# A four-layer image kernel on one core: the first scan chain's opening 160 steps interleaved with the tail of the gated layer

## The chip, the core and the metric

The kernel runs on one core of a Trainium2 chip, in one launch. The metric is the device time of that launch in microseconds, from the first to the last instruction on the core and the little that lies around it. Everything is in fp32.

The core has five engines that matter here. TensorE (PE, with its weight loads listed as PEld) multiplies matrices, VectorE (DVE) and ScalarE (ACT) work element by element, GpSimd (POOL) copies and adds, and SyncE (SP) issues nearly all the transfers. Each engine works through its own list of instructions in a fixed order.

## What is computed

Four residual layers on an input of 4 images, 48 channels, 256 x 256 pixels. Each layer adds f(groupnorm(x)) to x.

```python
# layer 0: channel attention; layer 1: gated tokens; layers 2 and 3: line scans
x = x + L0(_gn(x)); x = x + L1(_gn(x)); x = x + L2(_gn(x)); x = x + L3(_gn(x))

def step(w, b):                      # layers 2 and 3
    def f(carry, inp):
        nxt = inp + _conv1d(carry, w, b)      # 5 taps along the line, 48 -> 48 channels
        return (nxt, nxt)
    return f
_, d_rest = jax.lax.scan(step(down_w, down_b), d0, xs[1:])    # down the rows
_, u_rest = jax.lax.scan(step(down_w, down_b), u0, seq)       # up again
_, r_rest = jax.lax.scan(step(right_w, right_b), r0, ws[1:])  # to the right
_, l_rest = jax.lax.scan(step(left_w, left_b), l0, R[Ww - 2::-1])  # to the left
```

Layer 0 is a 1x1 and a 3x3 convolution, a 48 x 48 softmax attention over channels, and a projection. Layer 1 reinterprets the image as tokens of 48 numbers, applies two small dense products with GELUs, a layer norm, a 3x3 and a 1x1 convolution whose product gates half of the channels, and a last dense product. Layers 2 and 3 are chains: about a thousand line steps, each of which needs the result of the one before.

## The kernel before

`layers01` first forms the Gram products of layer 0 image by image, and from them folds attention and projection into one 3x3 convolution. This convolution is done in blocks of 16 rows, 16 blocks an image: `block(u)` gives six pieces, and one call of `conv()` (L631) runs three of them. The 16 blocks of image 0 run first; the other 48 are then mixed with the gated layer.

The gated layer (`gated_layer`, L649) works on 32 chunks, 8 an image, in a software pipeline: `tick(c)` (L906) finishes chunk c-2, works on chunk c and prepares chunk c+1. A tick calls `conv` four times, so two blocks go with a tick, until the list `todo` is empty. Before the ticks, four calls run two blocks ahead (L642). After `todo` is empty the remaining ticks are the lone gated chunks. In them `output` loads the residual x of the following chunk itself (L884, `load_x`, tile `xr`), where otherwise it comes at the head of the tick. All loads and stores of a chunk (`tok`, `xr`, `near`, the store at L889) go through SP's one queue.

`scans` then makes one generator for each of the two pairs of images. `chain(pair)` yields after each line step. `step` (L1059) is six matmuls in the source into two PSUM tiles, two VectorE additions that form the new line (`carry`), and two ScalarE writes (`keep`) into the slot that the input line came from. The first pass goes down 256 rows in eight groups of 32. Group n uses two slots, `halves[2n]` for the even rows and `halves[2n+1]` for the odd rows; a slot is 96 x 4096 floats, 1.5 MB, loaded in four transfers by `load_rows` (L1091) and then normalized in place by ScalarE at L1125. At the start of group n the list `halves` is filled up to index 2n+4 (L1142). When a group is finished its two slots are stored as `D[n]` (L1165).

Slots come from `take` (L1019) through a `Ring` of pools. `slots_a` has three buffers, in the memory that the convolution leaves; `slots_b` and `slots_c` have one each, in memory of the gated layer. The ring of pair 0 goes a, a, a, c, b and round again, so `halves[3]`, the odd rows of group 1, sits in c, and that is free only when the gated layer no longer uses it.

The order on each engine is fixed when the program is built. A planner walks through simulated time; among the instructions that are ready it takes the one with the lowest number, and numbers go up in the order in which the code emits. `tc.high_priority(offset=n)` sets the number back by n for what is emitted within it. `tc.issue_after(ins)` puts transfers in SP's queue behind `ins`, and waits for nothing else. `look` (L1033) is a tiny VectorE addition that is pinned in program order and reads a number written a few steps before. So the chains' first steps may move up among the lone gated chunks in two ways: as fill where the planner sees an engine free, or with a number that is set back. In the kernel before only the first two calls of `next(chains[0])` are set back (weights, the first two slots, then the first normalization and the loads of three more slots); the line steps have numbers after the gated layer's. Without a look go groups 0 and 1 of pair 0, layer 2 (L1159).

Of the kernel before, what the change touches and what calls it, by code (L numbers as in the profile page):

```python
# [1 line left out]

# [1 line left out]

# [12 lines left out]
B, C, H, W = 4, 48, 256, 256  # L17
# [4 lines left out]
R = 16  # L22
# [3 lines left out]
NK = W // (2 * KC)  # L26
LEAD = 4 * H - 32
# [32 lines left out]
class Coefs:  # L60


    def __init__(self, nc, pool, at, cst):
        self.nc, self.at = nc, at
        self.t = pool.tile([128, cst.shape[1]], F32, tag="cst", name="cst")
        nc.sync.dma_start(self.t, cst)
        self.eps = pool.tile([128, 1], F32, tag="eps", name="eps")
        nc.gpsimd.memset(self.eps, GN_EPS)
# [50 lines left out]
class Ring:  # L119


    def __init__(self, pools):
        self.pools = list(pools)

    def tile(self, *args, **how):
        self.pools.append(self.pools.pop(0))
        return self.pools[-1].tile(*args, **how)

# [2 lines left out]
def layers01(ctx, tc, x, x1, wqk, dwqk, wv, dwv, projT, temp, k, coef, coef1, gated, spare):  # L131
# [11 lines left out]
    nc = tc.nc  # L143
# [3 lines left out]
    p_small = ctx.enter_context(tc.tile_pool(name="a_ps", bufs=1, space=PSUM))  # L147
# [47 lines left out]
    halves = wp.tile([P, 2], F32, tag="halves", name="halves")  # L195
# [3 lines left out]
    w1 = wp.tile([P, 3, 3, P], F32, tag="w1", name="w1")  # L199
# [298 lines left out]
    banks = ctx.enter_context(tc.tile_pool(name="a_banks", bufs=5, space=PSUM))  # L498
# [63 lines left out]
    ends = []  # L562
# [68 lines left out]
    def conv():  # L631

        while ends:
            ends.pop(0)()
        if todo:
            u, q = todo.pop(0)
            if q == 0:
                made[u] = block(u)
            for piece in made[u][3 * q : 3 * q + 3]:
                piece()  # L640

    for _ in range(4):  # L642
        conv()
    for t in range(-1, n_ticks):
        for piece in tick(t, conv, not todo):
            piece()


def gated_layer(ctx, tc, banks, p_small, x1, x2, w1, w2, dw, ends, pw, cols, b2, k, coef1, coef2):  # L649

# [3 lines left out]
    nc = tc.nc  # L656
# [184 lines left out]
    def load_x(c, ip):  # L841

        if c >= len(items) or (c, ip) in xrs:
            return
        b, j = items[c]
        t = xrs[c, ip] = res.tile([P, 8, W], F32, tag=f"xr{ip}", name="xr")
        src = x1[b].rearrange("c (h w) -> c h w", w=W)[:, 2 * j * R : 2 * (j + 1) * R, :]
        src = src.rearrange("c (q i r) w -> i r c q w", i=2, r=2)
        for r in range(2):
            nc.sync.dma_start(t[r * C : (r + 1) * C], src[ip, r])  # L850

    def add_b2(c, ip):
        t = xrs[c, ip]
# [2 lines left out]
    def output(c, ip, alone):  # L856
# [27 lines left out]
        if alone:  # L884
            load_x(c + 1, ip)
# [76 lines left out]


@with_exitstack
def scans(ctx, tc, xs, out, wts, biases, dram, k, coefs, lead, spare):

# [10 lines left out]
    nc = tc.nc  # L979
# [7 lines left out]
    slots_a = pool("c_slot_a", 3)  # L987
    wp = pool("c_w", 1)
    work = pool("c_work", 1)
    slots_b = pool("c_slot_b", 1)  # L990
    slots_c = pool("c_slot_c", 1)
    slots_d = pool("c_slot_d", 5)
    p_small = pool("c_ps", 1, space=PSUM)
# [2 lines left out]
    sums = [spare, psum]  # L996
    zero = p_zero.tile([P, 1], F32, tag="zero", name="zero")
    nc.vector.memset(zero, 0.0)
    buffers = [Ring([slots_a] * 3 + [slots_c, slots_b]), Ring([slots_d] * 5)]
    NT = H // RT  # L1000
    NH = RT // 2
    CB = 2 * KC
# [19 lines left out]
    def chain(pair):  # L1022
# [10 lines left out]
        def look(place, fetched=None):  # L1033

            kept.append(place)
            old = [kept.pop(0)] if len(kept) > 3 else []
            for number in old + ([] if fetched is None else [fetched]):
                tc.keep_in_program_order(nc.vector.tensor_add(seen, zero, number))  # L1044

        def slot(name):
            return take(pair, f"{name}{pair}")

        def inner():
            return carry[at[0]][:, :, 1 : HP - 1]  # L1050
# [5 lines left out]
        def blocks(v):  # L1056
            return v.rearrange("p b (k w) -> p b k w", w=KC)
# [20 lines left out]
        def rows_view(t):  # L1078
            return t.rearrange("p (b k h w) -> p b k h w", b=2, k=NK, w=KC)
# [8 lines left out]
        def row(ts, r):  # L1088
            return rows_view(ts[r % 2])[:, :, :, r // 2, :]

        def load_rows(layer, n, r, t, k0, k1):  # L1091

            v = rows_view(t)
            for b in range(2):
                for q in range(2):
                    nc.sync.dma_start(
                        v[q * C : (q + 1) * C, b, k0:k1].rearrange("c k h w -> c k (h w)"),
                        xs[layer][pair][
                            r * C : (r + 1) * C, b, 2 * k0 + q : 2 * k1 - 1 + q : 2, n * NH : (n + 1) * NH, :
                        ].rearrange("c k h w -> c k (h w)"),  # L1100
                    )

        def layer_of(layer, first):
# [11 lines left out]
            for b in range(2):  # L1115
                t = home.tile([P, 2], F32, tag=f"biased{pair}{b}", name="biased", bufs=2)
# [5 lines left out]
            def norm(t, b):  # L1122
                v = by_batch(t)[:, b]
                g = biased[b]
                nc.scalar.activation(v, v, AF.Identity, bias=g[:, 1:2], scale=g[:, 0:1])  # L1125
# [10 lines left out]
            halves = list(first)  # L1136
            for n in range(NT):
                ahead_ = None
                for r in range(RT):
                    if r == 0:  # L1140
                        kept.clear()
                        while len(halves) < min(2 * n + 5, 2 * NT):  # L1142
                            t = slot("dn")
                            load_rows(layer, len(halves) // 2, len(halves) % 2, t, 0, NK)
                            halves.append(t)
                        if n + 1 < NT:
                            ahead_ = halves[2 * n + 2 : 2 * n + 4]
                    if ahead_ and r in (11, 14, 22, 25):
                        norm(ahead_[r // 22], r % 11 // 3)
                    inp = row(now, r)  # L1150

                    def keep(new, b):
                        nc.scalar.activation(inp[:, b], blocks(new[:, b]), AF.Identity, bias=bias[:, 0:1])  # L1153

                    if n == 0 and r == 0:
                        keep(inner(), slice(0, 2))
                    else:
                        step(layer, 0, inp, keep)
                    if pair or layer or n > 1:  # L1159

                        look(inp[:, 1, 0, 0:1])
                    yield
                if ahead_:
                    for r in range(2):
                        nc.sync.dma_start(D[n][r], now[r])  # L1165
                    now = ahead_
# [5 lines left out]
            for n in reversed(range(NT)):  # L1172
                ahead_ = None
                kept.clear()
                for r in reversed(range(RT)):
# [17 lines left out]
                    i = n * RT + r + 1  # L1193
# [9 lines left out]
                    else:  # L1203
                        step(layer, 0, place, keep)
                    look(place[:, 1, 0, 0:1])
                    yield
                    if n == 0 and r < 2:
# [63 lines left out]
            for n in range(NK):  # L1271
                ahead_ = None
                for w in range(CB):
# [27 lines left out]
                    if n + 1 < NK or w + 1 < CB:  # L1301
                        look(line[:, 1, 0:1], fetched[n * CB + w + 1][:, 1, 0:1])
# [91 lines left out]
            if layer == 0:  # L1394

                ends = []
# [14 lines left out]

        first = [slot("dn"), slot("dn")]
        for r in range(2):
            load_rows(0, 0, r, first[r], 0, NK)
        yield
        for layer in range(2):
            following = None
# [5 lines left out]
            first = following  # L1423

    def to_rows(pair, engines):
# [6 lines left out]
        for n in range(NY):  # L1432
# [9 lines left out]
            for half in range(2):  # L1442
# [12 lines left out]
                yield  # L1455

    chains = [chain(pair) for pair in range(NP)]

    with tc.high_priority(offset=1600):
        next(chains[0])  # L1460
    with tc.high_priority(offset=1400):
        next(chains[0])
    for i in range(1, lead):
        if i == lead - 2 * RT:
            next(chains[1])
        next(chains[0])
# [14 lines left out]
@with_exitstack  # L1481
def program(ctx, tc, a, out, at):
    nc = tc.nc
    const = ctx.enter_context(tc.tile_pool(name="const", bufs=1))
    dram = ctx.enter_context(tc.tile_pool(name="dram", bufs=1, space=DRAM))
    k = Coefs(nc, const, at, a["cst"])
    coefs = [
        [const.tile([P, 2], F32, tag=f"coef{layer}_{b}", name=f"coef{layer}_{b}") for b in range(B)]
        for layer in range(4)
    ]  # L1490
    spare = ctx.enter_context(tc.tile_pool(name="spare", bufs=2, space=PSUM))
    x1 = [dram.tile([C, HW], F32, tag=f"x1_{b}", name=f"x1_{b}") for b in range(B)]
    xs = [
        [dram.tile([P, 2, NK * 2, H // 2, KC], F32, tag=f"x{i}_{p}", name=f"x{i}_{p}") for p in range(NP)]
        for i in (2, 3)
    ]

    def gated(ctx, tc, banks, p_small):
        names = ("w1", "w2", "dw", "ends", "pw", "cols", "b2")
        return gated_layer(ctx, tc, banks, p_small, x1, xs[0], *(a[n] for n in names), k, coefs[1], coefs[2])  # L1500

    names = ("wqk", "dwqk", "wv", "dwv", "projT", "temp")
    layers01(tc, a["x"], x1, *(a[n] for n in names), k, coefs[0], coefs[1], gated, spare)
    scans(tc, xs, out, (a["c2w"], a["c3w"]), (a["c2b"], a["c3b"]), dram, k, coefs, LEAD, spare)


def _block_diag(m, n):
# [95 lines left out]
```

## Time and profile before

| what | value |
|---|---|
| device time, median of 3 runs | 8974.04 us (8972.58 to 8974.45) |
| the profiled execution's own time | 8983.88 us |
| its span, first to last instruction | 8982.1 us |
| PE busy | 8646.3 us, 96% |
| DVE, ACT, POOL busy | 4167.5, 3479.8, 1948.9 us |
| bytes moved by the transfer engines | 1390.64 MB, 155 GB/s over the span |
| scan matmuls L1067 | 48960 records, 5423.7 us busy |

Stages on the time line, with the line numbers that open and close them: the Gram products to about 1750 us, the convolution with the gated layer to about 3175 us (the last store of the convolution is issued at 3169.88 us), the lone gated chunks to about 3575 us, the scans to the end. The scan matmuls run from 3244.8 us.

How to read it: time that PE is not busy is what can be won, since PE's own work is the same in both kernels. A view by windows gives the busy time of each engine in a stretch, the mean TensorE clock that was granted there (PEclk, 1.00 is full), the share of the transfer engines that was busy, and the GB/s they moved. A scan matmul's record overlaps with its neighbours, so counts tell more than summed durations: where the chain runs alone 230 records fit in 25 us, which is 109 ns each, and a step has 12 records (48960 over 4080 steps), so 1.30 us.

### The profile page before, as it was taken

What the parts mean: (1) busy time and instruction counts of PE and PEld (TensorE: products, weight loads), DVE (VectorE), ACT (ScalarE), POOL (GpSimd) and SP (SyncE); (2) the same over time, 40 slices, a digit from 0 to 9 for tenths busy, and PEclk for the clock granted to TensorE, in tenths of its full rate; (3) what the DMA queues carried; (4) which work ended last, traced back from release to release, by engine and by line L of the source; (5) the groups of instructions that cost most, each with busy time, mean ns of one, the idle gap of its engine ahead of it and who ended that gap; (6) DMA issues with size and microseconds to landing.
All of it is one profiled execution on the core that took longest, in us unless ns stands there. A gap on an engine that the chain in (4) does not pass through costs nothing. (4 is left out here: it accounts for less than half of the span.)

```text
span 8982.1 us, 162711 instructions
## 1 busy us (share of the span) xinstructions
PE 8646.3 (96%) x62920; PEld 7223.1 (80%) x62920; DVE 4167.5 (46%) x15625; ACT 3479.8 (39%) x7023; POOL 1948.9 (22%) x3100
## 2 busy tenths in 40 slices
PE   6999999999999978999999999999999999999998
PEld 4777777533333335999999999999999999999998
DVE  3231110234555555445666444445666555444653
ACT  0010101123433455766601776666663003665610
POOL 0000000001111111001454000001445664101575
PEclk9999999999999988999999999999999999999998
DMA  7654323367888876765577664556656887867789
GB/s 152 132 125 94 74 61 77 82 140 160 173 181 182 182 165 162 168 138 143 155 190 190 152 139 120 141 135 141 169 146 175 216 220 181 198 172 191 210 176 183
DMA packets 1180233, 1390.64 MB, mean 155 GB/s; under 512 B 263184, under 2 KB 1107216, under 8 KB 1118784
## 3 DMA queue, kind: packets, MB, share of 16 engines
q1 hardware_dynamic: 1179360, 1379.90, 65.7%
q8 instruction: 493, 8.08, 0.4%
q14 instruction: 284, 2.33, 0.1%
q0 software_dynamic: 96, 0.33, 0.0%
HBM read 811.21 MB, written 509.61 MB: 147 GB/s over the span
## 5 line engine op out<-in xcount | busy, mean ns | idle before, releaser
L1067 PE MATMUL ps<-carry,w 96*96 96x128 f32 x48960 | 5423.7, 273 | 59.3 <-DVE carry L1071 29.1
L1067 PEld LDWEIGHTS ps<-carry,w 96*96 96x96 f32 x48960 | 5397.6, 163 | 95.0 <-issue 44.9
L1264 POOL COPY pre<-col 96x256 f32<-96x256 f32 x1020 | 657.5, 646 | 2682.2 <-DMA col<-last 1964.1
L1153 ACT ACTIVATE dn<-carry,b 96x128 f32<-96x128 f32 (+1 forms) x2044 | 769.0, 398 | 796.8 <-DVE carry L1071 789.0
L1291 ACT ACTIVATE lines<-carry,b 96x128 f32<-96x128 f32 (+1 forms) x2044 | 819.8, 402 | 583.9 <-DVE carry L1075 574.0
L1071 DVE TENSOR_TENSOR carry<-ps,dn 96x128 f32<-96x128 f32 x2280 | 653.2, 288 | 806.1 <-PE ps L1067 781.2
L1199 ACT ACTIVATE up<-carry,b 96x128 f32<-96x128 f32 x1792 | 719.5, 402 | 459.9 <-DVE carry L1071 459.6
L1075 DVE TENSOR_TENSOR carry<-ps,lines 96x128 f32<-96x128 f32 x2040 | 576.8, 286 | 562.8 <-PE ps L1067 552.9
L1075 DVE TENSOR_TENSOR carry<-ps,pre 96x128 f32<-96x128 f32 x2040 | 586.7, 288 | 457.6 <-PE ps L1067 402.4
L1071 DVE TENSOR_TENSOR carry<-ps,up 96x128 f32<-96x128 f32 x1792 | 516.0, 288 | 598.1 <-PE ps L1067 592.8
L1339 POOL TENSOR_TENSOR stage<-stage,carry 96x256 f32<-96x256 f32 x768 | 657.4, 857 | 470.4 <-DVE seen L1044 436.7
L581 PE MATMUL py<-x1n,wy 128*96 128x512 f32 x1536 | 703.1, 607 | 30.9 <-ACT x1n L541 28.4
L295 PE MATMUL acc<-xs,xt 128*96 128x288 f32 x2048 | 667.2, 408 | 0.0
L294 PE MATMUL acc<-xt 128*96 128x288 f32 x2048 | 666.8, 409 | 0.0
L581 PEld LDWEIGHTS py<-x1n,wy 128*96 128x96 f32 x1536 | 244.2, 165 | 454.7 <-issue 437.1
L279 DVE COPY xt<-pt 128x384 f32<-128x384 f32 x256 | 136.7, 555 | 849.0 <-PE pt L276 645.8
L261 ACT ACTIVATE xn<-raw,coef 96x2048 f32<-96x2048 f32 x64 | 133.7, 2095 | 987.0 <-PE pt L276 819.6
L296 PE MATMUL acc<-xt,xs 128*96 128x192 f32 x2048 | 502.1, 327 | 0.0
L296 PEld LDWEIGHTS acc<-xt,xs 128*96 128x96 f32 x2048 | 332.4, 165 | 154.5 <-issue 1.8
L295 PEld LDWEIGHTS acc<-xs,xt 128*96 128x96 f32 x2048 | 332.2, 165 | 151.4 <-issue 2.8
L604 DVE TENSOR_TENSOR y<-py,t 96x512 f32<-96x512 f32 x256 | 171.4, 678 | 593.3 <-PE py L590 584.4
L590 PE MATMUL py<-x2n,wy 64*96 64x512 f32 x1536 | 363.0, 601 | 0.0
(186 smaller groups left out, 5542.7 us busy)
## 6 DMA issues: line engine op xcount, KB each, us to landing
stage<-x SPq DMA_DIRECT2D x64, 1536.0 KB
dn<-x SPq DMA_DIRECT2D x240, 384.0 KB
R<-lines SPq DMA_DIRECT2D x60, 1536.0 KB
lines<-R SPq DMA_DIRECT2D x60, 1536.0 KB
D<-dn SPq DMA_DIRECT2D x56, 1536.0 KB
up<-D SPq DMA_DIRECT2D x56, 1536.0 KB
U<-up SPq DMA_DIRECT2D x224, 384.0 KB
col<-U SPq DMA_DIRECT2D x56, 1536.0 KB
```

Source lines behind the costliest of these rows:

```text
L294: nc.tensor.matmul(acc[0], lhsT=xt[:, h + 2, :], rhs=xt[:, here, :], start=first, stop=last)
L295: nc.tensor.matmul(acc[1], lhsT=xt[:, h + 2, :], rhs=xs[:, here, :], start=first, stop=last)
L296: nc.tensor.matmul(acc[2], lhsT=xs[:, h + 2, :], rhs=xt[:, past, :], start=first, stop=last)
L581: nc.tensor.matmul(ps, lhsT=held["w"][0][:, dx], rhs=x1n[:, 2 * c : 2 * c + 2, dx : dx + W], start=dx == 0, stop=False)
L1067: nc.tensor.matmul(ps, lhsT=w_sb[layer][:, way, j, :], rhs=old[:, i, j : j + W // 2], start=j == 0, stop=j == 2)
L1071: nc.vector.tensor_add(new[:, i].rearrange("p (k w) -> p k w", w=KC), ps.rearrange("p (k w) -> p k w", w=KC), inp[:, i])
L1075: nc.vector.tensor_add(new[:, i], ps, inp[:, i])
L1153: nc.scalar.activation(inp[:, b], blocks(new[:, b]), AF.Identity, bias=bias[:, 0:1])
L1199: nc.scalar.activation(place[:, b], blocks(new[:, b]), AF.Identity, bias=bias[:, 1:2])
L1264: nc.gpsimd.tensor_copy(t, cols_view(block)[:, :, w % 2, :, w // 2])
L1291: nc.scalar.activation(line[:, b], new[:, b], AF.Identity, bias=bias[:, 2:3])
L1339: nc.gpsimd.tensor_add(to, to, new)
```

## The change

Four things change together.

- The convolution runs eight calls (four blocks) ahead of the first tick, not four. It is thus done a tick earlier, and there are 13 lone ticks rather than 12.
- The steps of pair 0 in the first five groups (160 calls) have numbers set back by 1400, call by call.
- The first eleven slots of pair 0 all come from the three buffers of `slots_a`; only then does the ring go c, b, a, a, a. Eleven slots are `halves[0]` to `halves[10]`, so groups 0 to 4 need no memory of the gated layer.
- The first two slots' loads stand in SP's queue behind the load of x (`xr`, second half) of chunk 21, the third slot's behind that of chunk 22.

Looks now begin at group 5 of that pass, where they began at group 2.

```diff
 class Ring:
-    def __init__(self, pools):
+    def __init__(self, pools, first=()):
         self.pools = list(pools)
+        self.first = list(first)
     def tile(self, *args, **how):
+        if self.first:
+            return self.first.pop(0).tile(*args, **how)
         self.pools.append(self.pools.pop(0))
...
-    for _ in range(4):
+    for _ in range(8):
         conv()
...
         for r in range(2):
-            nc.sync.dma_start(t[r * C : (r + 1) * C], src[ip, r])
+            loads[c, ip] = nc.sync.dma_start(t[r * C : (r + 1) * C], src[ip, r]).ins
...
-    buffers = [Ring([slots_a] * 3 + [slots_c, slots_b]), Ring([slots_d] * 5)]
+    buffers = [Ring([slots_c, slots_b] + [slots_a] * 3, [slots_a] * 11), Ring([slots_d] * 5)]
...
+        def behind(n):
+            return nullcontext() if pair else tc.issue_after(loads[B * H // (2 * R) - 11 + n, 1])
...
-                            load_rows(layer, len(halves) // 2, len(halves) % 2, t, 0, NK)
+                            with behind(1) if layer == 0 and len(halves) == 2 else nullcontext():
+                                load_rows(layer, len(halves) // 2, len(halves) % 2, t, 0, NK)
...
-                    if pair or layer or n > 1:
+                    if pair or layer or n > 4:
                         look(inp[:, 1, 0, 0:1])
...
         for r in range(2):
-            load_rows(0, 0, r, first[r], 0, NK)
+            with behind(0):
+                load_rows(0, 0, r, first[r], 0, NK)
...
     with tc.high_priority(offset=1600):
         next(chains[0])
-    with tc.high_priority(offset=1400):
-        next(chains[0])
-    for i in range(1, lead):
+    for i in range(160):
+        with tc.high_priority(offset=1400):
+            next(chains[0])
+    for i in range(160, lead):
         if i == lead - 2 * RT:
             next(chains[1])
         next(chains[0])
```

More of the change, by code (lines that the diff above doesn't have):

```diff
@@ L1 @@
-from contextlib import ExitStack
+from contextlib import ExitStack, nullcontext
 import numpy as np
@@ L646, in layers01, with gated_layer @@
             piece()
-def gated_layer(ctx, tc, banks, p_small, x1, x2, w1, w2, dw, ends, pw, cols, b2, k, coef1, coef2):
+def gated_layer(ctx, tc, banks, p_small, x1, x2, w1, w2, dw, ends, pw, cols, b2, k, coef1, coef2, loads):
     nc = tc.nc
@@ L964, in scans @@
 @with_exitstack
-def scans(ctx, tc, xs, out, wts, biases, dram, k, coefs, lead, spare):
+def scans(ctx, tc, xs, out, wts, biases, dram, k, coefs, lead, spare, loads):
     nc = tc.nc
@@ L1496, in program @@
     ]
+    loads = {}
     def gated(ctx, tc, banks, p_small):
         names = ("w1", "w2", "dw", "ends", "pw", "cols", "b2")
-        return gated_layer(ctx, tc, banks, p_small, x1, xs[0], *(a[n] for n in names), k, coefs[1], coefs[2])
+        return gated_layer(ctx, tc, banks, p_small, x1, xs[0], *(a[n] for n in names), k, coefs[1], coefs[2], loads)
     names = ("wqk", "dwqk", "wv", "dwv", "projT", "temp")
     layers01(tc, a["x"], x1, *(a[n] for n in names), k, coefs[0], coefs[1], gated, spare)
-    scans(tc, xs, out, (a["c2w"], a["c3w"]), (a["c2b"], a["c3b"]), dram, k, coefs, LEAD, spare)
+    scans(tc, xs, out, (a["c2w"], a["c3w"]), (a["c2b"], a["c3b"]), dram, k, coefs, LEAD, spare, loads)
 def _block_diag(m, n):
```

## The prediction

> **What bounds the kernel now.** I read the page first, then windows around the place where the slices dip, then SP's list and PE's waits there.
>
> ```profile
> PE 8646.3 (96%) x62920; PEld 7223.1 (80%) x62920; DVE 4167.5 (46%) x15625; ACT 3479.8 (39%) x7023; POOL 1948.9 (22%) x3100
> ...
> PE   6999999999999978999999999999999999999998
> ```
>
> PE is the bound nearly everywhere; the 7 and the 8 cover 3144 to 3593 us, where the lone gated chunks run. The windows (columns: stretch, length, busy and count of PE, PEld, DVE, ACT, POOL, then granted clock, share of the DMA engines, GB/s) say how much is lost there:
>
> ```profile
> 1750.00:3175.00 1425.00, 1342.04 (x4783) 496.29 (x4782) 685.48 (x1167) 506.93 (x483) 176.89 (x408) 0.98 0.79 169
> 3175.00:3575.00 400.00, 315.71 (x1541) 169.63 (x1540) 230.54 (x502) 207.32 (x283) 71.19 (x77) 0.84 0.74 164
> 3575.00:4250.00 675.00, 674.38 (x6144) 673.27 (x6143) 332.84 (x1530) 456.08 (x1063) 34.75 (x54) 1.00 0.66 153
> ...
> 3175.00:3245.00 70.00, 35.50 (x127) 14.66 (x126) 25.12 (x56) 26.32 (x26) 11.11 (x11) 0.68 0.97 180
> 3245.00:3575.00 330.00, 280.21 (x1415) 154.97 (x1415) 205.42 (x446) 180.99 (x258) 60.08 (x66) 0.87 0.70 161
> ```
>
> PE idles 84.3 us in these 400 us: 34.5 before the chain's first step, 49.8 beside it. The clock is down too. After 3575 us the chain alone fills PE (674.38 of 675), so whatever steps are not done earlier cost their 1.30 us each there and no more: only idle time and slow clock can be won. The first hole is made in SP's queue:
>
> ```profile
> 3171.51 1.47 SPq L850 DMA_DIRECT2D xr<-x  x1
> 3173.08 23.71 SPq L1096 DMA_DIRECT2D dn<-x  x12
> 3196.83 4.25 SPq L850 DMA_DIRECT2D xr<-x  x3
> ```
>
> Twelve loads of three slots take 23.7 us of issuing and stand before the chunk's residual x. PE's waits in 3175 to 3250, then in 3250 to 3470, then in 3470 to 3580 (total, times, longest):
>
> ```profile
> PE pout L868 <- DVE y L879: 21.2, 1, 21.2
> PE ptok L751 <- POOL pairs L745: 9.7, 1, 9.7
> ```
> ```profile
> PE ptok L751 <- DVE y L879: 16.3, 5, 3.5
> ```
> ```profile
> PE ps L1067 <- DVE carry L1071: 16.2, 7, 4.0
> ```
>
> The first two are that missing x, and token loads behind it. The third comes once a tick. The last is the chain itself standing at PE's head: at 3481 us the odd rows of group 1 are just loaded and being normalized, and everything behind that step on PE waits too.
>
> **What the skill says.** "TensorE: Matmul & The Clock Gate", Part 1, says that a PE left idle for a few microseconds falls to half its clock; the trace agrees (0.68 in the first 70 us, 1.00 once the chain runs alone). Part 2 of that page, on loading weights, says that matmuls themselves stay in program order; the 16.2 us fit. "DMA: Bandwidth & Descriptors", Two DMAs through the same engine are not ordered, says that a dependent transfer has to wait for the first one's completion before it is issued. In the trace that wait is visible, and its price (the two D stores of group 1, then the first load behind them):
>
> ```profile
> 3583.53 1.66 SPq L1165 DMA_DIRECT2D D<-dn  x2
> 3592.41 14.52 SPq L1096 DMA_DIRECT2D dn<-x  x8
> ```
>
> 8.9 us from store to load, 1.8 us for each load, with the gated layer gone. "Perfetto Trace Analysis", Optimization Strategy, recommends interleaving stages with different limits; the combined stage, 94% busy on PE, agrees.
>
> **The change part by part.** All sums are against the profiled execution (8983.9 us; 9.8 above the median).
>
> *Convolution ahead.* Two blocks move from tick 21 to before tick -1. The same matmuls and the same nine transfers a block (seven loads, two stores) on SP. A combined tick loses about 83/23 = 3.6 us of PE idle (1425 - 1342 over 23 ticks), and one such tick becomes a lone tick. Nothing, 5 either way. Chunk 24's image is ready a tick earlier; no wait of before shows that this was late.
>
> *First loads behind x.* Eight loads follow chunk 21's x, four more chunk 22's. They still take 1.9 us each on SP, 16 and 8 us, and what stands behind is the store of a chunk, its successor's tokens and the near rows; those have slack of 10 to 20 us in a steady tick (tokens issued at 3315.2, relayed after 3345). So the waits of 21.2 and 9.7 us go. But two lone ticks now run before the chain has data (x of chunk 21 is loaded in the second of them, then 16 us of loads and four normalizations of 2.08 us), so I expect the chain to start near 3230 us instead of 3245, and PE to be thin until then. The tick 3251 to 3280, which had only 38 scan records, kept PE busy 24.1 of 28.8 us; without those (4.1 us) it is 70%. Of the 34.5 us idle I take 18 as won, 8 to 30.
>
> *Steps set back.* A step has ten instructions, a lone tick about 118, so 1400 numbers are the 12 last ticks and 140 steps, 11 to 12 a tick, where before there are 5 to 6 (60 to 72 records). The three-odd us that PE waits each tick for `y` (22.1 us in 3250 to 3470 with the two single waits) are where VectorE does sixteen additions; carries with an older number can now go between them. I take 12 of 22 as won, 0 to 20. In 3470 to 3575, 20.1 us are idle; the chain no longer waits there for memory c, which came free at 3470 with the last transpose: 12 won, 0 to 18. Clock: 0.84 over 400 us becomes perhaps 0.9; I take 10, 0 to 25. POOL receives nothing. The 96 looks that go are 145 ns each on a VectorE that is half idle: nothing.
>
> Won in all: 18 + 12 + 12 + 10 = 52 us.
>
> *Three buffers.* This is the new wait. With three buffers, group n holds two slots, and only the even rows of group n+1 are loaded ahead. The odd rows need the buffer of `halves[2n]`, so: last step, store D (8.9 us to landing), four loads (7.3 us), landing, half a normalization (2.1 us): 20 us, and 35 with the gated layer's transfers between (DMA share 0.66 in its ticks) and D[n][1] already in the rings. Only the first row of group n+1 can run meanwhile. There are four such boundaries, 0-1 to 3-4; that of 4-5 has slots b and c. Queued behind the waiting load on SP are the gated chunk's `xr`, `near` and `tok`; behind the waiting step on PE is everything. Before, no row load waits on a store while chunks run, save in group 1. Price of one boundary: 30 us with the gated work alone at 70% busy is 9 us; PE at a standstill because its fixed order expects the step sooner than the transfers allow, 6 (what 3481 to 3490 shows for one late load, 3.1 + 3.2); slow clock after it, 4. That is 19, and four are 76 us. Bounds: 6 each if a chunk is always ready (24), 30 each if the stall is bare (120); below nothing is excluded, as before had the same rows to load with memory to spare later.
>
> Sum: 8983.9 - 52 + 76 = 9007.9 for a profiled execution, 9.8 less for the median: 8998 us, 0.27% slower.
>
> **The rivals.**
>
> *Covered boundaries (faster).* If the planner's order and the chunks' slack cover the stalls, each boundary costs 6, and the gains are those above: 8974 - 52 + 24 = 8946; with the upper gains (18 + 18 + 16 + 16 = 68) 8930. For it: the combined stage holds 94% with transfers at 0.79. Against: a boundary stops the chain for most of a tick, and the last may fall where chunks have run out, so nothing covers it. It decides where a boundary costs under 13 us (52 over 4).
>
> *A wash.* Boundaries at 13 us and gains of 52, or both small: 8974, within 18 us. For it: both sums come out of the same 84 us.
>
> *SP's queue as the bound.* Each load that waits for a store holds back the chunk's x and near rows, as the twelve loads did at 3173. With 12 us more a boundary 48 come on top: 9046. For it: 21.2 us from a single case. Against: SP is idle for 20 us in each tick, and these loads come one slot at a time.
>
> *The change doesn't do what it says:* the steps don't move up since the chain lacks data; then it has only the delayed first loads, some 8970. Small.
>
> **How the numbers follow.** What this kernel's measurement can tell from no change is about 0.2%, 18 us. The forecast (boundaries cost more than the filled gaps) 0.45, its own range 8992 to 9025; queue as the bound 0.11; covered boundaries 0.28; wash, with the idle change in it, 0.16. Faster 0.28, within 0.16, slower 0.56. The range, 8936 to 9046, leaves out the upper gains and the worst queue.
>
> **What would show it.** Right: PE waits `ps` on `carry` of several us in four places some 100 us apart, each after a D store and a row load; no wait of over 10 us on `y` at the stage's start; 140 or so steps done when the last chunk ends, and a stage about 480 us long. Wrong: PE's idle time from 3150 us until the chain is alone under 60 us, with short waits at the boundaries; or x loads late behind a waiting row load.

## The result, and the profile after

The changed kernel takes 9132.88 us, median of 4 runs (9126.90 to 9136.76), where the kernel before, measured beside it, takes 8974.25 (8972.58 to 8981.89): 1.0174 times, 95% interval 1.0157 to 1.0192, 158.6 us slower. The forecast was 8998 us with a range to 9046. The profiled execution has a span of 9135.0 us, 152.9 more than before.

First the page of the changed kernel: busy time by engine, and two rows of the 40 slices. (Line numbers moved: the scan matmuls of L1067 are L1074 now, the carry additions L1078, the row loads L1103, the store of a slot L1173, `xr` L853.)

```profile
PE 8780.4 (96%) x62920; PEld 7312.2 (80%) x62920; DVE 4163.8 (46%) x15538; ACT 3484.9 (38%) x7025; POOL 1947.2 (21%) x3100
...
PE   6999999999999988899999999999999999999998
...
PEclk9999999999999977899999999999999999999999
```

PE has the same 62920 instructions and is busy 134.1 us longer. Only 18.8 of the 152.9 us are new idle time; the rest is the same work done more slowly, so idle time alone doesn't tell what is lost here. The two 7s in the row of the clock say where. The windows of the changed kernel (stretch, length, busy and count of PE, PEld, DVE, ACT, POOL, granted clock, share of the DMA engines, GB/s):

```profile
3210.00:3885.00 675.00, 589.46 (x2937) 412.60 (x2935) 286.63 (x717) 324.67 (x536) 64.04 (x71) 0.75 0.60 127
...
3175.00:3575.00 400.00, 341.62 (x1654) 233.30 (x1649) 157.39 (x375) 189.22 (x306) 42.06 (x42) 0.73 0.60 122
...
3350.00:3400.00 50.00, 43.49 (x172) 35.49 (x171) 12.28 (x30) 23.71 (x35) 1.81 (x3) 0.50 0.37 84
3500.00:3550.00 50.00, 44.10 (x183) 38.50 (x183) 9.40 (x31) 17.08 (x35) 4.07 (x3) 0.50 0.23 46
3900.00:3950.00 50.00, 50.00 (x459) 49.99 (x458) 24.00 (x110) 38.65 (x83) 0.00 (x0) 1.00 0.57 146
```

The stage of the lone chunks now lasts until about 3885 us, 310 more than before. In 3175 to 3575 us PE is busier than before (341.6 for 315.7 us) and yet does little more: 1654 records for 1541. In the third and fourth line the chain runs with hardly any chunk work at a clock of 0.50; the last line is the same chain, later, at 1.00. PE's own timeline in such a stretch (start, duration, operation, count, idle time before it and what ended that):

```profile
3377.70 2.88 PE L1074 MATMUL ps<-carry,w 96*96 96x128 f32 x12 [0.45 <-DVE carry L1078]
3381.03 2.88 PE L1074 MATMUL ps<-carry,w 96*96 96x128 f32 x12 [0.45 <-DVE carry L1078]
3384.35 2.88 PE L1074 MATMUL ps<-carry,w 96*96 96x128 f32 x12 [0.45 <-DVE carry L1078]
```

One step of twelve records takes 3.32 us, with one wait for a carry in it; before, a step where the chain runs alone took 1.30 us. PE's waits from 3100 to 4300 us (total, times, longest) and SP's list at the start and at the first boundary:

```profile
PE ps L1074 <- DVE carry L1078: 62.1, 75, 5.1
PE ph L701 <- DVE y L882: 11.2, 4, 2.8
PE ptok L754 <- POOL pairs L748: 8.4, 2, 8.1
```
```profile
3211.54 2.33 SPq L853 DMA_DIRECT2D xr<-x  x2
3213.96 15.48 SPq L1103 DMA_DIRECT2D dn<-x  x8
...
3323.15 1.66 SPq L1173 DMA_DIRECT2D D<-dn  x2
3332.04 13.85 SPq L1103 DMA_DIRECT2D dn<-x  x7
```

The 21.2 us wait for `y` of before is gone, as forecast; of the 9.7 us wait for `pairs` 8.1 are still there. The carry waits are 75, not four long ones. At the first boundary between two groups the forecast 8.9 us from store to load are there (3323.15 to 3332.04; 10.2 at the next, 8.8 and 8.9 at the two after that), but PE idles only 7.3 us in 3321 to 3360.

Why a carry is waited for in each step is told by PE's fixed order and by the numbers, both read from the built program. First PE's list in the changed kernel (line, operation, tile written and tile read, count); each PSUM tile is one half of a step:

```
L1074 Matmult ps_15875<-carry_1 x1     half 1 of step s
L1074 Matmult ps_15881<-carry_2 x3     half 0 of step s+1
L1074 Matmult ps_15875<-carry_1 x2     half 1 of step s, the rest
L1074 Matmult ps_15887<-carry_2 x1     half 1 of step s+1: needs the carry of the line above
```

Then the planner's counter around each of the 160 calls:

```
call  before  inside           after
0     12982   11582 to 11605   12982
1     12982   11582 to 11592   12982
2     12982   11582 to 11592   12982
...
159   12982   11582 to 11592   12982
```

The set-back ends with its block, and the counter returns to where it was; so the next call starts from 11582 again. All steps share the same ten numbers (25 of the 160 calls take a few more: the first of each group and four others in each). The last two matmuls of half 1 have higher numbers than the next step's half 0, so half 0 goes first as soon as its carry is there, and half 1 then follows straight behind the half that it depends on. Of the first 160 steps 146 have their halves interlaced so; in the kernel before none has.

### The profile page after: what moved, and what is told of

The parts are those of the page before. It is cut to its first block, busy times and chain, and to the rows that moved or that the text cites. A ratio compares the mean times of both kernels' runs of the same rounds, so it can differ in the third digit from the quotient of the medians.

```text
span 9135.0 us, 162710 instructions
## 1 busy us (share of the span) xinstructions
PE 8780.4 (96%) x62920; PEld 7312.2 (80%) x62920; DVE 4163.8 (46%) x15538; ACT 3484.9 (38%) x7025; POOL 1947.2 (21%) x3100
## 4 chain that ended last, share of the span: by engine, by line
PE 87%; DMA 5%; DVE 3%; ACT 1%; issue 1%; SPq 1%; POOL 1%; DVEq 0%; POOLq 0%; ACTq 0%
PE ps L1074 57%; PE py L584 6%; PE acc L297 6%; PE acc L298 5%; PE acc L299 4%; PE py L593 3%; DMA tok<-x 1%; DMA stage<-x 1%; PE pt L279 1%; PE pout L871 1%; PE ptok L754 1%; PE ph L701 1%; DMA sx<-in_x 1%; PE ptap L354 0%; DVE st L1388 0%
## 5 line engine op out<-in xcount | busy, mean ns | idle before, releaser
L1074 PEld LDWEIGHTS ps<-carry,w 96*96 96x96 f32 x48960 | 5486.1, 165 | 228.8 <-DVE carry L1078 97.6
L1074 PE MATMUL ps<-carry,w 96*96 96x128 f32 x48960 | 5547.1, 276 | 111.4 <-DVE carry L1078 74.0
L1078 DVE TENSOR_TENSOR carry<-ps,dn 96x128 f32<-96x128 f32 x2280 | 653.6, 288 | 992.7 <-PE ps L1074 932.2
L1078 DVE TENSOR_TENSOR carry<-ps,up 96x128 f32<-96x128 f32 x1792 | 516.1, 288 | 595.9 <-PE ps L1074 591.3
```

The costliest lines, as they stand in the source:

```text
L1074: nc.tensor.matmul(ps, lhsT=w_sb[layer][:, way, j, :], rhs=old[:, i, j : j + W // 2], start=j == 0, stop=j == 2)
L1078: nc.vector.tensor_add(new[:, i].rearrange("p (k w) -> p k w", w=KC), ps.rearrange("p (k w) -> p k w", w=KC), inp[:, i])
```

## The experiments

**The numbers.** One edit to the changed kernel, so that numbers rise from step to step:

```diff
-    for i in range(160):
-        with tc.high_priority(offset=1400):
-            next(chains[0])
+    with tc.high_priority(offset=1400):
+        for i in range(160):
+            next(chains[0])
```

> All 160 calls under one set-back of 1400, so that numbers go up from step to step; buffers, loads and convolution as in the change. If the equal numbers of all 160 steps are the cause (each step's first half outranks the end of the step before, VectorE's latency lies bare, the clock stays at half), the time falls by 100 us or more, to 8930 to 9020, with no stretch of 30 us at clock 0.50. If three buffers are the cause, as the prediction has it, the boundaries are the same and it stays at 9080 or above.

Measured: 8977.88 us, ratio to before 1.0003 (0.9994 to 1.0011), as the first of the two cases. No step has interlaced halves in PE's list any more, and the whole loss is gone. Every other part of the change (three buffers, loads behind x, convolution ahead) is still in this kernel, so together, with rising numbers, they neither cost nor win anything that shows. This is the kernel that the prediction reckoned with.

But this edit also lets the chunks pass between the steps again. To part order from precedence, the same block was set back by 3400, ahead of every lone chunk:

> One set-back of 3400: numbers go up, and yet every one of the 160 steps outranks all of the lone chunks, as in the change. If the order of the two halves is what costs, it is within 40 us of the run with 1400 (8930 to 9050) and steps take 1.3 us. If it is the chunks being starved by the chain, it stays near the change, 9080 to 9140. Three buffers: 9080 or above.

Measured: 9010.65 us, 1.0040 (1.0025 to 1.0055). So precedence over all chunks costs 33 us beside the kernel set back by 1400. The windows show it at the end of the stage, first with 3400, then with 1400:

```profile
3600.00:3650.00 50.00, 39.62 (x163) 15.70 (x161) 32.18 (x58) 25.38 (x30) 12.59 (x13) 0.80 0.77 179
3650.00:3700.00 50.00, 34.46 (x141) 16.16 (x142) 24.76 (x47) 25.13 (x29) 5.44 (x7) 0.79 0.68 147
```
```profile
3600.00:3650.00 50.00, 45.37 (x294) 29.93 (x293) 31.27 (x71) 31.22 (x51) 4.07 (x5) 1.00 0.47 99
3650.00:3700.00 50.00, 39.29 (x181) 22.57 (x178) 34.90 (x89) 22.11 (x30) 7.12 (x12) 0.85 0.93 225
```

With 3400 the 160 steps are used up and the last chunks stand alone, with PE 70 to 80% busy at a clock of 0.8.

Two other numberings. One keeps a block around each call, with an offset of 0 (shared numbers without precedence):

> Each call in its own block with a set-back of 0: all 160 steps share one range of numbers, but behind the chunks, so they only fill gaps. If the order of the halves costs by itself, steps take 2 to 3.3 us where the chain is alone and the time is above 9050, up to 9250. If precedence over the chunks is what costs, it is at 8960 to 9010.

Measured: 9172.36 us, 1.0226 (1.0204 to 1.0248). Sharing alone is enough. No chunk work is left in the two windows of this kernel that follow, and yet they differ:

```profile
3650.00:3700.00 50.00, 50.00 (x452) 49.85 (x451) 21.92 (x77) 38.92 (x82) 0.00 (x0) 1.00 0.76 161
3850.00:3900.00 50.00, 43.35 (x182) 38.13 (x183) 8.64 (x30) 14.11 (x32) 0.00 (x0) 0.50 0.00 1
```

In this kernel the second pair's chain comes early. By the count of scan records (927 lie ahead of the first window) the windows can be found in PE's list: of the 226 matmuls of the first, 133 are the second pair's, between the steps of the first pair; all 91 of the second are the first pair's. So interlaced steps run without a gap where another chain fills their waits. The second window leaves 6.65 us of 50 idle at half the clock, with the DMA engines at 0.00, so no transfer is to blame.

The other numbering sets back the first call only, as before, and keeps the rest of the change:

> The first call set back by 1400 as before, the other 159 with their own numbers; three buffers, late first loads and the convolution ahead are kept. If the equal numbers are the cause, 8950 to 9000. If the buffers' boundaries are, 9030 or above, with PE waits of several us for carry after each D store.

Measured: 9041.94 us, 1.0076 (1.0061 to 1.0091), in the range given for the buffers: with only the first call set back, three buffers do cost, and PE waits for a carry up to 17.1 us at a time.

**The order alone.** In the changed kernel, shared numbers and all, the first matmul of each step is tied behind the last one of the step before:

```diff
                 for j in range(3):
-                    nc.tensor.matmul(
+                    with tc.issue_after(last_mm[0]) if last_mm and not i + j else nullcontext():
+                        mm = nc.tensor.matmul(
...
+                if pair == 0 and layer == 0 and way == 0:
+                    last_mm[:] = [mm.ins]
```

> The changed kernel with one thing added: the first matmul of every step of the first pair's first layer is tied behind the last matmul of the step before it on the same engine, so the two halves keep their order although all 160 steps still share the same ten numbers and still come ahead of the last twelve gated ticks. Theory A (the swapped halves are the loss: a half follows straight behind the half whose carry it needs, 0.45 us bare in every step, and the clock stays at 0.50): some 9010 us, as the kernel whose chain outranks every lone chunk in the right order; steps of about 1.35 us wherever the chain runs bare. Theory B (the equal precedence is the loss, the order of the halves only comes with it): 9100 us or more, stretches with clock 0.50 stay.

Measured: 9013.36 us, 1.0044 (1.0031 to 1.0056), theory A. 119.5 us of the loss are the order of the halves, and what is left over one block of 1400 (35.5 us) is what precedence cost above. PE's timeline of this kernel, where the chain runs bare:

```profile
3399.78 20.38 PE L1077 MATMUL ps<-carry,w 96*96 96x128 f32 x181
```

181 records without a gap in 20.38 us, 113 ns each.

The reverse, in the 3400 kernel with rising numbers: the last two matmuls of half 1, its addition and its `keep` are emitted behind half 0 of the next step.

```diff
+                if not early or not i:
+                    some(range(3))
+                    rest()
+                    continue
+                last = pending.pop()() if pending else None
+                some((0,))
+                pending.append(second)
...
+                if count[0] % RT == RT - 1 or count[0] == 160:
+                    pending.pop()()
```

> The kernel whose one block of numbers that rise puts the chain ahead of every lone chunk (measured 9010.7 with the halves in order), with one thing changed: the halves of the first 160 steps are swapped by hand, so that the last two matmuls of half 1 and what follows them come behind half 0 of the next step. Numbers are no longer shared by any two steps. Theory A (the swapped halves alone make the loss): 9130 us within 30, steps of 3.3 us with clock 0.50 where the chain runs bare. Theory B (shared numbers do something else besides): under 9060 us.

Measured: 9133.52 us, 1.0178 (1.0163 to 1.0194): the time of the changed kernel, with 146 interlaced steps as there. The swap costs 122.9 us here. Its timeline has the same lines:

```profile
3366.66 2.87 PE L1080 MATMUL ps<-carry,w 96*96 96x128 f32 x12 [0.45 <-DVE carry L1087]
3369.99 2.88 PE L1080 MATMUL ps<-carry,w 96*96 96x128 f32 x12 [0.45 <-DVE carry L1087]
```

The same swap where chunks may pass between the steps (one block, 1400):

> The halves swapped by hand as before, in the kernel with one block of rising numbers from 1400 back (8977.9 in order), where the chunks keep their place between the steps. Theory A (the swap costs only where no chunk's work stands between the steps): under 9060 us, most of the chain beside chunks at clock 1.00. Theory B (the swap costs the same anywhere, as in the kernel whose chain comes first: 123 us): about 9100 us.

Measured: 9160.83 us, 1.0205 (1.0189 to 1.0220). Both theories were too low. The swap costs 183 us here: PE waits for a carry 108 times for 73.7 us from 3100 to 4000, and the chain is at clock 0.50 still at 3800 to 3850 us. In this kernel too the chain is left bare for long: 167 of the 172 records in 3350 to 3400 us are its own. Where a chunk's matmuls do stand in each wait, from 3405.68 to 3417.01 us, PE doesn't wait, and twelve records go from 2.88 us to 1.50. That chunks may pass between the steps is thus no protection; something has to stand in every wait. Nor do order and precedence simply add: with the halves swapped, precedence saves 27 us (9160.8 to 9133.5) where it costs 33 with the halves in order.

**Clock or wait?** The kernel with an offset of 0 shows bare interlaced steps at both clocks, before and after a wait of 18.4 us (windows, then PE's timeline between them). By the count of records these are steps of the first pair alone, with their halves interlaced in PE's list:

```profile
3780.00:3816.00 36.00, 27.85 (x216) 24.07 (x216) 10.29 (x36) 14.18 (x36) 0.00 (x0) 1.00 0.00 1
3843.00:3939.00 96.00, 83.34 (x348) 73.30 (x348) 16.59 (x58) 27.15 (x60) 0.00 (x0) 0.50 0.03 5
```
```profile
3814.54 1.55 PE L1074 MATMUL ps<-carry,w 96*96 96x128 f32 x12 [0.45 <-DVE carry L1078]
...
3838.51 1.60 PE L1074 MATMUL ps<-carry,w 96*96 96x128 f32 x6 [18.39 <-DVE carry L1078]
3843.32 2.85 PE L1074 MATMUL ps<-carry,w 96*96 96x128 f32 x12 [3.21 <-DVE carry L1078]
```

At 1.00 an interlaced step takes 2.00 us (216 records in 36 us), at 0.50 it takes 3.31. So of the 2.02 us by which 3.32 exceeds 1.30, 0.70 are the wait and 1.32 the clock. And the wait alone doesn't bring the clock down: 18 steps with it ran at 1.00 in a row. But once the clock is down, 29 steps with the same wait ran at 0.50 without getting it back. In the changed kernel a stretch at 0.50 likewise begins at or behind each of the four boundaries that the prediction named, where PE's longest waits are 2.8, 3.2, 5.1 and 3.1 us, and ends where chunk work fills several waits in a row.

Does filling the wait bring the clock back? At half the clock the wait is some 0.66 us (3.32 less twelve times 0.222, the spacing of the records in the next timeline; the 0.45 that the timelines show is what their modelled ends leave). Matmuls on the weights alone were put into the wait, in the swapped 3400 kernel, first two, then four a step:

```diff
+                with tc.issue_after(last) if last else nullcontext():
+                    for _ in range(2):
+                        nc.tensor.matmul(
+                            ps[:, :P], lhsT=w_sb[0][:, 0, 0, :], rhs=w_sb[0][:, 0, 1, :], start=True, stop=True
+                        )
```

> The kernel with the halves swapped by hand, and in each of the 160 steps two more matmuls of 96x96 on the weights alone, ahead of half 1, where PE otherwise stands for 0.45 us; the true matmuls overwrite what they leave. Theory A (most of the price is the clock, which stays at half as long as that gap is there): the gaps close, the clock is 1.00 beside the chain, a bare step takes some 1.8 us in place of 3.3, and the time falls although work is added: 9030 to 9070 us. Theory B (the price is the wait itself): the added matmuls change nothing for the better, 9130 us or more and bare steps of 3.3 us or longer.

Measured: 9169.98 us, 1.0217 (1.0203 to 1.0231), theory B by its time. The timeline (L1106 are the added matmuls) and one window of this kernel:

```profile
3620.83 0.84 PE L1106 MATMUL ps<-w 96*96 96x96 f32 x4
3621.48 2.88 PE L1080 MATMUL ps<-carry,w 96*96 96x128 f32 x12
3624.15 0.85 PE L1106 MATMUL ps<-w 96*96 96x96 f32 x4
```
```profile
3600.00:3650.00 50.00, 50.00 (x222) 44.89 (x221) 8.81 (x29) 19.68 (x33) 3.07 (x4) 0.50 0.33 78
```

PE has no idle time in these 50 us, and the clock is still 0.50. But the step is as long as before, 3.32 us: 2.67 for the twelve and 0.65 for the four added records, which just fill the wait at half the clock. Elsewhere in the same trace a carry was done at 3533.92 us, and the matmul that needs it started at 3533.97: the step is still as long as its carry takes. (From 3350 to 3400 us, where it came in with the clock up, this kernel has 304 records at 0.87.) Four added matmuls, 1.3 us at half the clock, outlast the wait:

> As the kernel with two added matmuls a step (9170.0), with four of them, so that PE has work for longer than the wait for the carry at either clock (0.66 us at the full one, 1.33 at half). Theory A (even a rest of a wait in every step keeps the clock at half): with none left the clock beside the bare chain is 1.00, a bare step takes some 2.0 us, and the time is 9050 to 9110. Theory B (it isn't the wait for the carry that holds the clock down): steps of 4.0 us with clock 0.50, over 9200 us.

Measured: 9110.73 us, 1.0149 (1.0135 to 1.0163): theory A, though 0.7 us above the range given. It is 59.3 us less than with half of the added work and 22.8 less than with none (9105.0 to 9113.5 for 9117.8 to 9137.6). The same two views:

```profile
3520.48 0.92 PE L1106 MATMUL ps<-w 96*96 96x96 f32 x8
3521.24 1.48 PE L1080 MATMUL ps<-carry,w 96*96 96x128 f32 x12
3522.55 0.27 PE L754 MATMUL ptok<-cst,pairs 128*128 128x128 f32 x1
3522.72 0.92 PE L1106 MATMUL ps<-w 96*96 96x96 f32 x8
```
```profile
3500.00:3550.00 50.00, 50.00 (x412) 41.43 (x411) 22.73 (x61) 21.93 (x45) 1.45 (x3) 1.00 0.11 23
```

The clock is 1.00. A step of twelve scan records, eight added ones and one of the gated layer comes every 2.24 us (3520.48 to 3522.72), shorter than the 3.32 us of twelve records without help. What the kernel still loses against the ordered one (9110.7 less 9010.7, 100 us) is of the size of the added work itself: 160 times 0.76 us, the length of the added records above, would be 122, by estimate.

**The other parts of the change.** The convolution eight calls (four blocks) ahead, alone in the kernel before; where the texts below say eight and four blocks, they mean calls of `conv()`:

> The kernel before with the convolution eight blocks ahead in place of four, nothing else. Theory A (nothing waits for these blocks): 8974 us within 9. Theory B (one combined tick becomes a lone tick, or the start gets longer): over 8983 us.

Measured: 8970.27 us, 0.9993 (0.9985 to 1.0001): nothing that shows. With the first loads behind x besides:

> The kernel before with the convolution eight blocks ahead and the first loads of the chain behind the residual x of two chunks; five buffers and one step set back, as before. Theory A (the 21.2 and 9.7 us waits for x at the start of the lone stage go, and the chain starts no later): some 8956 us, 18 less, with PE's idle time in 3175 to 3245 us about half of 34.5. Theory B (the chain starts later by what is saved, or the idle time turns up later in the stage): 8974 us within 9.

Measured: 8997.87 us, 1.0027 (1.0017 to 1.0036): 28 us more than with the convolution alone, neither theory. PE's idle time in 3175 to 3245 us did fall as theory A has it, from 34.5 to 22.0, but the time did not. Scan records alone (PE, PEld, DVE, clock, DMA, GB/s), in the kernel before and then in this one:

```profile
3250.00:3300.00 50.00, 7.85 (x62) 7.14 (x62) 2.87 (x11) 0.89 0.75 179
3350.00:3500.00 150.00, 35.16 (x255) 32.37 (x256) 11.85 (x44) 0.89 0.69 167
```
```profile
3250.00:3300.00 50.00, 35.83 (x298) 35.27 (x296) 14.02 (x49) 0.95 0.65 127
3350.00:3500.00 150.00, 3.17 (x24) 2.82 (x24) 0.55 (x2) 0.80 0.68 156
```

Here the chain runs through nearly all of group 0 at once and then has nothing to do until memory c is loaded (first at 3490.42 us, where the kernel before loads it at 3470.34); meanwhile the chunks stand alone at a clock of 0.80. Where the edge is taken out of the kernel with one block:

```diff
-            return nullcontext() if pair else tc.issue_after(loads[B * H // (2 * R) - 11 + n, 1])
+            return nullcontext()
```

> The kernel with one block around all 160 calls (8977.9), without the edge that puts the first loads of the chain behind the residual x of two chunks. Theory A (that edge frees PE of the two waits at the start of the lone stage and is worth what was forecast for it): 8996 us, 18 more. Theory B (what PE idles there is the lone chunks' own, or the later start of the chain takes it back): 8978 us within 9, or less.

Measured: 8971.72 us, 0.9996 (0.9987 to 1.0004), theory B. The wait comes back (PE's waits from 3150 to 3260 us):

```profile
PE pout L871 <- DVE y L882: 14.7, 1, 14.7
PE ptok L754 <- POOL pairs L748: 6.1, 1, 6.1
```

and costs nothing: PE is busy 81.2 of these 110 us, 75.0 with the edge (and 74.6 in the kernel before). With the edge one chunk earlier (`- 12` in place of `- 11`):

> The kernel with one block around all 160 calls (8977.9), with the first loads behind the residual x of the two chunks before those of the change. If the chain starts a chunk earlier without a new wait for x, some 10 steps move into the gaps at the start of the stage: 8966 us. If the waits for x of the kernel before come back: 8978 us or more.

Measured: 8982.35 us, 1.0004 (0.9996 to 1.0012); no gain.

Five buffers in place of three, in the kernel with one block:

```diff
-    buffers = [Ring([slots_c, slots_b] + [slots_a] * 3, [slots_a] * 11), Ring([slots_d] * 5)]
+    buffers = [Ring([slots_a] * 3 + [slots_c, slots_b]), Ring([slots_d] * 5)]
```

> The changed kernel with one precedence block around all 160 calls, so that numbers rise, and the five buffers of before in place of three. Theory A (three buffers cost a wait at each of four boundaries, some 8 us of idle PE each by the trace of the changed kernel): 8978 - 30 = 8948 us. Theory B (the boundaries are covered by chunks once the halves are in order, or five buffers give the same waits elsewhere): 8978 us within 10.

Measured: 9057.46 us, 1.0088 (1.0074 to 1.0102): 80 us lost where 30 were to be won. Scan records, and SP's loads of rows:

```profile
3250.00:3300.00 50.00, 41.26 (x350) 39.67 (x349) 16.39 (x57) 0.99 0.39 69
3350.00:3500.00 150.00, 0.00 (x0) 0.00 (x0) 0.00 (x0) 0.80 0.73 166
```
```profile
3314.08 16.21 SPq L1103 DMA_DIRECT2D dn<-x  x8
...
3515.57 2.44 SPq L1103 DMA_DIRECT2D dn<-x  x4
```

After group 0 the chain stands for over 150 us: the next slot is in memory c. So three buffers are what lets early steps go on, and early steps are what makes three buffers bearable: without precedence (the kernel with its own numbers, 9041.9, against the five-buffer kernel with both other parts, 8997.9) they cost 44 us, with it they save 80. (The 44 hold the `look`s of groups 2 to 4 too, which only the second of the two has.)

A last try for a kernel that beats both, free loads with the block set back by 1200:

> The kernel with one block and free first loads (8971.7) with the block 1200 back in place of 1400: the last steps of the 160 come later, beside the last chunks. If steps are spread better over the lone ticks: 8950 to 8965 us. If the gaps at the start of the stage and at the boundaries are what remains: 8972 us within 9.

Measured: 9003.78 us, 1.0032 (1.0020 to 1.0043), worse than both cases. The chain comes later (30 scan records by 3250 us, 222 with 1400), and PE idles 39 us from 3150 to 3250 in place of 29; the rest of the loss was not traced. The best of all, 8970.3 and 8971.7, can't be told from the kernel before.

## Why the prediction was wrong, point by point

- *Steps set back*, the step that failed: "A step has ten instructions, a lone tick about 118, so 1400 numbers are the 12 last ticks and 140 steps, 11 to 12 a tick". This takes numbers to go up from call to call. The diff opens a block for each call, and the counter goes back when a block ends: 160 steps share ten numbers. Two things follow that have no term in the sum. The halves interlace (119.5 us by the tied kernel, 122.9 by the swap alone), and the chain outranks all twelve ticks at once (33 to 36 us). Together they are the 155 us between the changed kernel (9132.9) and the kernel with one block (8977.9). The parts depend on the order in which they are taken: at the chunks' own place the interlacing alone costs 183 us, and precedence then takes 27 back.
- The size of the first fits the trace: from 3350 us on, in stretches of 25 us whose clock is at or under 0.60, the changed kernel has 804 scan records, 67 steps. 67 times 2.02 us is 135, an estimate from above, since some of these steps have chunk work in their waits.
- *Clock*: forecast to rise from 0.84 to about 0.9, 10 us won. It fell to 0.73 in the same 400 us. What the term has nothing for is a loop that stays at half the clock once it is there.
- *Convolution ahead*, nothing: right (8970.3, interval to 1.0001).
- *First loads behind x*, 18 won: of the two waits the 21.2 us one went, as said, the other stayed (8.1 of 9.7 us). The chain started at 3232 us for the 3230 forecast, but the time didn't fall. It isn't a gain with rising numbers (8977.9 with the edge, 8971.7 without, intervals overlap) and a loss of 28 with the buffers and numbers of before. In place of that wait stands thin chunk work while the chain waits for its data: from 3150 to 3260 us PE is busy 74.6 us before and 75.0 with the edge. The prediction saw that and still took half as won.
- *Three buffers*, four times 19 lost: the mechanism is there (store, 8.9 us, load), the size isn't. In the changed kernel PE idles 7.3, 8.8, 10.1 and 7.1 us around these four boundaries and 4.2 at the next, where the prediction had 15 of its 19 for idle time; what a boundary costs the kernel with one block was not measured by itself. And the term has the other sign where steps come early: the prediction knew the wait for memory c at 3470 us and priced it at 12 us, but the five buffers cost 80 when the chain gets there 150 us sooner.
- *Set-back and three buffers together*, 34 won and 76 lost in the sum, so 42 more: the kernel with one block and free loads against the one with the convolution ahead alone, 8971.7 to 8970.3, are 1 us apart. With numbers as I had read them, the rival called a wash would have held. (The upper gains of its other rival, 68 us, are not the tops of the ranges given, 30, 20, 18 and 25; nothing hangs on it.)
- *SP's queue as the bound* (9046): no; no chunk waits over 2.8 us for `y` in the changed kernel.
- *The change doesn't do what it says*: this was the case, but the other way round from what I priced. The steps moved up too far, and out of order.

Slower was right in direction by luck: none of the causes given is the one that was found.

What stays open: why exactly the clock stayed at half with two added matmuls, where the records show PE busy without a break. That the step was still as long as its carry takes suggests a rest of waiting too short for the records; four added matmuls released the clock, so it isn't the kind of work. How long a wait brings the clock down in the first place is not shown either, nor whether interlaced steps would have kept the clock with buffers enough for the boundaries not to stop the chain; no run has both.

## What to carry to other kernels

A set-back that ends with its block gives every pass of a loop the same numbers, and passes of a dependent chain then interlace: put the block around the loop, and read the fixed order of the bounding engine for each tile's matmuls before thinking about time. A wait far under a microsecond in each step of a short dependent loop can cost three times its length (2.02 us for 0.70 here) when the TensorE clock has once fallen and the loop doesn't get it back; read the granted clock, and compare the count of records in equal stretches, for PE's busy time alone hides it. A smaller ring and an earlier start belong together: try each without the other before pricing either.

## What the runs showed of the hardware

The Trainium skill, "TensorE: Matmul & The Clock Gate", Part 1, says that throttled is the default state and that about 3.4 us of sustained activity release the clock. The runs agree in that a full PE gets its clock back: the same loop with the wait overfilled runs at 1.00. Two things were not expected. The loop with one wait of some 0.7 us in each step has two states that last: 2.00 us a step at 1.00 for 36 us, though PE is busy only 27.85 of them, and 3.31 us a step at 0.50 for 96 us, with PE busy 83.34 (the two windows of the kernel with an offset of 0). And a loop of 3.32 us with PE busy in 50.00 of 50.00 us by its records stayed at 0.50 too. Here the measurement goes further than the page: busy by the records was not enough.

And adding work made a kernel faster: 640 more matmuls, 22.8 us less.
